# A graph layer's dense passes in plain fp32 instead of two 12-bit parts in float32r

## The chip, the cores and the metric

One core of one Trainium2 chip. The time is that of one launch in device microseconds; the kernel before was run three times.

## The reference

Two GraphSAGE layers, a linear layer, a residual and a layer norm, on 12500 nodes with 256 features and 200000 edges sorted by destination. The destinations are drawn as 12500 u^2, so the first nodes receive most edges.

```python
def _sage_conv(x, src, dst, W_l, b_l, W_r):
    msgs = x[src]
    agg = jax.ops.segment_sum(msgs, dst, num_segments=N_NODES)
    deg = jax.ops.segment_sum(jnp.ones((src.shape[0],), x.dtype), dst, num_segments=N_NODES)
    mean = agg / jnp.maximum(deg, 1.0)[:, None]
    return mean @ W_l + b_l + x @ W_r
...
h = jax.nn.relu(_sage_conv(x, src, dst, W1_l, b1, W1_r))
h = jax.nn.relu(_sage_conv(h, src, dst, W2_l, b2, W2_r))
out = _layernorm(x + (h @ W3 + b3))
```

## The kernel before

The sum over edges is made in two ways.

- **Hot nodes** (the first 1792 in layer one, 2304 in layer two) have so many edges that a dense product pays. For a range of destination nodes the kernel keeps a matrix of counts (how often node s sends to node d), in uint8, by source block: 98 blocks of 128 source nodes. `count` (line 881) builds it: DVE makes 0/1 matrices ("pick", line 908), TensorE multiplies them (lines 930 and 934), ACT or DVE copies the sums to the uint8 counts (lines 944 and 948). `products` (line 841) then runs a **pass**: for every source block, rows (features) as the stationary operand times the counts of 512 destination nodes, widened to 32 bits by ACT (`widened`, line 833), added up in two PSUM banks, `dense_ps` for the first 128 features and `beside_ps` for the others. A pass over 256 nodes (a half pass) uses one bank. Layer one has three full passes and a half one, layer two four and a half one.
- **The other nodes** are gathered: a **round** is four indirect DMAs on POOL's queue (line 286) of 128 rows each, and matmuls by 0/1 matrices that add the rows of a node (lines 298 and 314), added to a ring of sums by DVE (line 328). There are 474 rounds.

A **block** of 128 destination nodes whose sums are ready goes through the layer's own matmuls, which are plain fp32 with 256 columns (`sage`, lines 1123 and 1125; in layer two also line 1207 and the layer norm).

Precision of the passes: the rows are used as two float32r parts, the upper 12 bits of the mantissa (a bitwise and) and the rest. Layer one gets the parts from a stage of its own, `splitting` (line 784): x is loaded to the place of the counts not yet made, DVE splits two blocks at a time (lines 812 and 813), and the parts are stored to the DRAM tensor `x2_d`. Layer two gets them where a block of h is made: `exact` (lines 760 and 761) and a second store, to `h2_d`. `loaded` (line 775) brings one block's two parts, 256 KB, into one of five tiles. A block in a full pass is four matmuls: two parts, two halves of the features.

The order of the work is written out by a planner at build time. `layer` (line 645) goes through the rounds and gives each a room in us (5.05 in layer one, 5.0 in layer two); it fills a round with pieces of blocks and with dense work taken from a generator, each priced on PE, DVE and ACT, until the costliest engine has used up the room. Prices are written in the code, among them

```python
def product_cost(width):
    on_pe, on_act = (1.0, 0.62) if width == DN else (0.6, 0.33)
...
COST_DEGREES, COST_REST, COST_SPLIT = (0.5, 0.25, 0.0), (0.0, 0.0, 0.3), (0.0, 1.25, 0.0)
...
yield 1.75, 1.65, 1.1     # a block of the first layer: its own matmuls, DVE with the splitting, ACT
```

Each engine then runs its instructions in that order. `stages_1` and `stages_2` (lines 1055 and 1067) say which counting runs beside which pass; layer one ends with a pass alone, and layer two begins with one.

Of the kernel before, what the change touches and what calls it, by code (L numbers as in the profile page):

```python
# [8 lines left out]
F32 = mybir.dt.float32  # L9
F32R = mybir.dt.float32r  # L10
F16 = mybir.dt.float16
BF16 = mybir.dt.bfloat16
I32 = mybir.dt.int32
U16 = mybir.dt.uint16
U8 = mybir.dt.uint8
# [12 lines left out]
P = 128  # L28
# [23 lines left out]
def by_runs(  # L52
# [89 lines left out]
    h_d = dram.tile([NB * P, D], F32, name="h_d")  # L142
    x2_d = dram.tile([P, NB, 2, D], F32, name="x2_d")
    h2_d = dram.tile([P, NB, 2, D], F32, name="h2_d")
    CW = DN + WIDEST
# [471 lines left out]

    split = keep.tile([P, 2, 2, D], F32, name="split")
    assert NB * CW % 4 == 0
    counts_flat = [keep.tile([P, NB * CW], U8, name=f"counts{i}") for i in range(2)]  # L620
    counts = [t.rearrange("p (b d) -> p b d", b=NB) for t in counts_flat]

# [134 lines left out]

    def exact(t, s):

        nc.vector.tensor_scalar(s[:, 0].bitcast(I32), t.bitcast(I32), -4096, None, op0=OP.bitwise_and)  # L760
        nc.vector.tensor_tensor(s[:, 1], t, s[:, 0], op=OP.subtract)

    STREAMS = 4
# [8 lines left out]

    N2, WIDE = 5, 4

    def loaded(b, back, table):

        rows = rows_pool.tile([P, 2, D], F32, name="rows", bufs=N2)
        load = nc.sync.dma_start(rows, table[:, b])
        freed(load, back)
        if table is h2_d:  # L780
            tc.add_manual_dep(load.ins, rows_after, LANDED, reason="the first layer's last gathers")
        return rows

    def splitting():

        size = 2 * 2 * D
        bufs = NB * CW // 4 // size
        flat = counts_flat[1].bitcast(F32)
        raw = {}

        def fetched(u):
            t = flat[:, u // 2 % bufs * size:(u // 2 % bufs + 1) * size].rearrange("p (b k d) -> p b k d", b=2, k=2)
            whole = min(2, (N - u * P) // P)
            loads = []
            if whole < 2:
                left = N - (u + whole) * P
                nc.vector.memset(t[:, whole, 1], 0.0)
                loads.append(nc.sync.dma_start(t[:left, whole, 1], x[(u + whole) * P:N]))
            if whole:
                loads.append(nc.sync.dma_start(t[:, :whole, 1], x[u * P:(u + whole) * P].rearrange(  # L800
                    "(b p) d -> p b d", p=P)))
            if u < 2 * bufs:
                for load in loads:
                    tc.add_manual_dep(load.ins, strips[-1], LANDED, reason="the gathers' tables first")
            return t

        for b in range(0, NB, 2):
            for u in range(b, min(b + 2 * (bufs - 3), NB), 2):
                if u not in raw:
                    raw[u] = fetched(u)  # L810
            s = raw.pop(b)
            nc.vector.tensor_scalar(s[:, :, 0].bitcast(I32), s[:, :, 1].bitcast(I32), -4096, None, op0=OP.bitwise_and)
            nc.vector.tensor_tensor(s[:, :, 1], s[:, :, 1], s[:, :, 0], op=OP.subtract)
            nc.sync.dma_start(x2_d[:, b:b + 2], s)
            yield COST_SPLIT

# [16 lines left out]
    def widened(counted):  # L833
        wide = rows_pool.tile([P, DN], F32, name="wide", bufs=WIDE)
        if len(counted.shape) > 2:
            nc.scalar.copy(wide.rearrange("p (b d) -> p b d", b=2).bitcast(F32R), counted)
        else:
            nc.scalar.copy(wide.bitcast(F32R), counted)  # L838
        return wide

    def products(n0, width, counts_of, table, into):


        half = width < DN
        ps = [pool.tile([P, DN], F32, name=name)
              for pool, name in ((dense_pool, "dense_ps"), (beside_pool, "beside_ps"))[:width // 256]]
        if half:
            nc.tensor.matmul(ps[0], lhsT=zeros_b, rhs=steps[:, :DN], start=True, stop=False)
        rows, counted, wide = {}, {}, {}
        for b in range(0, NB, 2):  # L850
            for u in range(b, min(b + N2, NB)):
                if u not in rows:
                    rows[u] = loaded(u, b - (u - N2), table)
                    counted[u] = counts_of(u) if not half or u % 2 == 0 else None
            for u in range(b, min(b + 4, NB)):
                if u not in wide:
                    wide[u] = wide[u - 1] if half and u % 2 else widened(counted[u])
            for u in (b, b + 1):
                for k in range(2):
                    for c in range(NC):  # L860
                        own = rows[u][:, k, c * P:(c + 1) * P].bitcast(F32R)
                        if half:
                            a = u % 2 * width
                            nc.tensor.matmul(ps[0][:, c * width:(c + 1) * width], lhsT=own,  # L864
                                             rhs=wide[u][:, a:a + width].bitcast(F32R), start=False,
                                             stop=u == NB - 1 and k == 1 and c == NC - 1)
                        else:
                            nc.tensor.matmul(ps[c], lhsT=own, rhs=wide[u].bitcast(F32R),  # L868
                                             start=u + k == 0, stop=u == NB - 1 and k == 1)
# [127 lines left out]
    COST_DEGREES, COST_REST, COST_SPLIT = (0.5, 0.25, 0.0), (0.0, 0.0, 0.3), (0.0, 1.25, 0.0)  # L997

# [56 lines left out]
    def stages_1(waiting):  # L1055

        into = [rows_pool.tile([P, NC, 256], F32, name=f"sums_{i}", bufs=1) for i in range(2)]
        nc.vector.memset(counts[0][:, :, DN:], 0.0)
        yield [counting(3), (degrees(HOT1 // P), 12.0), (splitting(), NB // 2 * max(COST_SPLIT))]
        nc.vector.memset(counts[1][:, :, DN:], 0.0)  # L1060
        yield [passed(waiting, 1536, 256, held(0, 256), x2_d, into), counting(2),
               moving(count_d[1], counts[0][:, :, :256])]
        yield [passed(waiting, 1024, 512, held(1), x2_d, into), counting(1), moving(count_d[0], counts[1])]
        yield [passed(waiting, 512, 512, held(0), x2_d, into), counting(0)]
        yield [passed(waiting, 0, 512, held(1), x2_d, into)]

    def stages_2(waiting):

        into = sums_a, sums_b
        yield [passed(waiting, 512, 512, held(0), h2_d, into)]  # L1070
        yield [passed(waiting, 0, 512, held(1), h2_d, into), moving(counts[0][:, :, :256], count_d[1]), counting(4)]
        yield [passed(waiting, 1024, 512, streamed(count_d[0]), h2_d, into), counting(5)]
        yield [passed(waiting, 1536, 512, held(0), h2_d, into)]
        yield [passed(waiting, 2048, 256, held(1, 256), h2_d, into)]

# [73 lines left out]
    def first_block(b, agg=None):  # L1149
# [85 lines left out]
    nc.sync.dma_start(biases[:, 0], b2[None, :].to_broadcast([P, D]))  # L1235
    sums_a, sums_b = tables[:, :NC * 256].rearrange("p (c d) -> p c d", c=NC), split[:, 0]
    w3_sb = split[:, 1]
    nc.sync.dma_start(w3_sb, w3.rearrange("(c p) f -> p c f", p=P))
# [7 lines left out]

    layer(Gathers(h_d, True), last_block, 5, staged(stages_2), 5.0, 14)

# [368 lines left out]
```

## Time and profile before

| what | us |
|---|---|
| median of three runs | 3097.36 |
| lowest, highest | 3088.63, 3106.94 |
| the profiled execution | 3104.8 |
| its span in the trace | 3103.0 |

The mean granted clock of TensorE was 0.897. A row of a group gives the line, the engine, the operation, the tiles it writes and reads, their shapes and the count, then busy us and the mean ns of one, then the idle time of the engine just before them and what ended most of it. A matmul's record lasts from its start to its modelled end, so neighbours overlap. A row of waits gives who waited for whom: total us, times, longest.

### The profile page before, as it was taken

Reading aid. Unit: us, or ns where it says so; the run is one execution under the profiler, and the core shown is the slowest. Engines: PE = TensorE matmul, PEld = TensorE weight load, DVE = VectorE, ACT = ScalarE, POOL = GpSimd, SP = SyncE. Lnnn points to the kernel's source line nnn. Section 1 sums busy time; section 2 is a strip of 40 time slices with the busy share of each in tenths; the row PEclk is TensorE's granted clock in tenths of the full one; section 3 lists DMA queues with packets and bytes.
Section 4 is the critical chain, followed back from the end, with each engine's and each line's share of the span. In section 5 each row is a group of like instructions: output and inputs, shape, how many; then the busy total and the mean of one; then the engine's idle time right before and its main releaser. Section 6 shows DMA issues by size and latency. Waiting matters only on the chain.

```text
span 3103.0 us, 45692 instructions
## 1 busy us (share of the span) xinstructions
PE 2412.6 (78%) x13753; PEld 1604.2 (52%) x13753; DVE 1525.2 (49%) x4554; ACT 1384.4 (45%) x2794; POOL 1851.4 (60%) x1906
## 2 busy tenths in 40 slices
PE   3356888888878788888876888887888888887776
PEld 1123555555544555556554555554555566566644
DVE  6764766656666666643232124444444343344344
ACT  0236666666622666644332443554444423333321
POOL 6546666556655666656654665665666556666653
PEclk7567999999999999989988998998998899989988
DMA  4893877756655555567756875766677657677843
GB/s 116 301 348 109 260 228 232 252 183 200 188 183 164 174 165 177 170 187 245 241 178 198 258 229 177 219 215 184 209 226 230 192 173 219 212 222 236 263 130 90
DMA packets 366615, 634.88 MB, mean 205 GB/s; under 512 B 85371, under 2 KB 173081, under 8 KB 366361
## 3 DMA queue, kind: packets, MB, share of 16 engines
q1 hardware_dynamic: 271011, 382.42, 38.3%
q0 software_dynamic: 91008, 248.63, 26.7%
q8 instruction: 115, 1.88, 0.2%
q10 hardware_dynamic: 4342, 0.80, 0.2%
q14 instruction: 139, 1.14, 0.1%
HBM read 544.85 MB, written 86.78 MB: 204 GB/s over the span
## 4 chain that ended last, share of the span: by engine, by line
PE 63%; issue 9%; DVE 8%; another core or an unknown queue 7%; DMA 6%; ACT 5%; DVEq 1%; POOL 0%; ACTq 0%; SPq 0%; POOLq 0%
PE dense_ps L868 10%; PE beside_ps L868 10%; PE count_ps L930 9%; PE part_ps L298 8%; PE block_ps L1123 5%; PE block_ps L1125 5%; PE sum_ps L314 5%; PE block_ps L1207 3%; PE block_ps L1094 3%; ACT counts L944 3%; PE dense_ps L864 3%; PE count_ps L934 2%; DMA rows<-h_d 2%; DMA x_d<-counts 1%
## 5 line engine op out<-in xcount | busy, mean ns | idle before, releaser
L286 POOL DMA_INDIRECT got<-in_x_dram,src_t x988 | 983.6, 996 | 646.1 <-issue 241.3
L286 POOL DMA_INDIRECT got<-h_d,src_t x908 | 865.6, 953 | 573.9 <-issue 226.4
L930 PE MATMUL count_ps<-pick,low 128*128 128x490 bf16 x1360 | 453.8, 376 | 333.8 <-ACT counts L944 139.1
L944 ACT CAST counts<-count_ps 128x490 f32 (+2 forms) x852 | 581.2, 682 | 232.3 <-PE count_ps L934 52.4
L868 PE MATMUL dense_ps<-wide,rows 128*128 128x512 f32 x1372 | 637.7, 465 | 46.5 <-ACT wide L838 16.3
L868 PE MATMUL beside_ps<-wide,rows 128*128 128x512 f32 x1372 | 565.7, 412 | 0.0
L838 ACT CAST wide<-counts 128x512 fp32r<-128x512 uint8 x588 | 359.6, 621 | 455.8 <-PE beside_ps L868 188.9
L868 PEld LDWEIGHTS dense_ps<-wide,rows 128*128 128x128 f32 x1372 | 276.6, 202 | 187.3 <-issue 99.5
L908 DVE TENSOR_SCALAR pick<-steps,tables 128x686 bf16<-128x686 f16 (+3 forms) x792 | 319.0, 416 | 105.2 <-PE count_ps L930 38.6
L298 PE MATMUL part_ps<-got,one 128*32 128x257 f32 (+1 forms) x3792 | 331.7, 424 | 22.8 <-DMA got<-h_d,src_t 12.4
L930 PEld LDWEIGHTS <-low 128*128 128x128 bf16 x1360 | 152.0, 117 | 318.2 <-issue 161.6
L948 DVE CAST counts<-count_ps 128x196 f32 (+2 forms) x316 | 208.5, 660 | 179.8 <-PE count_ps L930 46.9
L868 PEld LDWEIGHTS beside_ps<-wide,rows 128*128 128x128 f32 x1372 | 275.8, 201 | 40.1 <-ACT split L876 0.3
L308 ACT COPY some<-part_ps 128x257 f32<-128x257 f32 (+1 forms) x340 | 127.0, 374 | 351.1 <-PE part_ps L298 102.9
L314 PEld LDWEIGHTS sum_ps<-two,some 128*128 128x128 f32 x1360 | 223.7, 215 | 89.4 <-issue 39.4
L242 DVE TENSOR_TENSOR one<-lo_t,lane_b 128x128 f32<-128x128 bf16 x474 | 134.8, 286 | 267.1 <-PE part_ps L298 81.6
L314 PE MATMUL sum_ps<-two,some 128*128 128x128 f32 x1360 | 238.7, 303 | 32.2 <-ACT some L308 12.8
L328 DVE TENSOR_TENSOR sums<-sums,sum_ps 128x256 f32 x340 | 139.7, 411 | 250.0 <-PE beside_ps L868 88.7
L1133 DVE TENSOR_TENSOR own<-block_ps,biases 128x256 f32<-128x256 f32 x196 | 82.9, 423 | 312.3 <-remote 101.8
L298 PEld LDWEIGHTS part_ps<-got,one 128*32 128x32 f32 x3792 | 78.5, 112 | 191.1 <-issue 167.9
L934 PE MATMUL count_ps<-aft,low 128*128 128x98 bf16 x659 | 169.0, 256 | 0.0
L1130 ACT COPY sums<-zero 128x256 f32<-128x256 f32 x164 | 66.4, 405 | 224.6 <-PE block_ps L1125 74.3
(199 smaller groups left out, 2904.8 us busy)
## 6 DMA issues: line engine op xcount, KB each, us to landing
rows<-h_d SPq DMA_DIRECT2D x490, 256.0 KB
rows<-x_d SPq DMA_DIRECT2D x392, 256.0 KB
x_d<-counts SPq DMA_DIRECT2D x49, 512.0 KB
h_d<-split SPq DMA_DIRECT2D x98, 256.0 KB
got<-in_x_dram,src_t POOLq DMA_INDIRECT x988
got<-h_d,src_t POOLq DMA_INDIRECT x908
h_d<-own SPq DMA_DIRECT2D x98, 128.0 KB
h_sb<-h_d SPq DMA_DIRECT2D x98, 128.0 KB
```

The lines of the kernel that those rows point to most:

```text
L286: rows = nc.gpsimd.indirect_dma_start(out=g[:, j, :D], out_offset=None, in_=self.table, in_offset=bass.IndirectOffsetOnAxis(ap=src_t[:, e: ...
L298: strip = nc.tensor.matmul(part_ps[j * W:(j + 1) * W, :width], lhsT=one[:, j], rhs=g[:, j, :width], start=r == 0, stop=r == n - 1)
L314: nc.tensor.matmul(sum_ps[:, c], lhsT=some[:, c * P:(c + 1) * P], rhs=two, start=True, stop=True)
L838: nc.scalar.copy(wide.bitcast(F32R), counted)
L868: nc.tensor.matmul(ps[c], lhsT=own, rhs=wide[u].bitcast(F32R), start=u + k == 0, stop=u == NB - 1 and k == 1)
L908: nc.vector.tensor_scalar(r[:, :w * NB], steps[:, :w * NB], key_t[g][:, t - lo_g:t - lo_g + 1], None, op0=OP.is_equal)
L930: nc.tensor.matmul(ps[:, :(b - a) * NB], lhsT=s, rhs=r[:, a * NB:b * NB], start=j == 0, stop=j == n_in - 1 and alone)
L934: nc.tensor.matmul(ps[:, :NB], lhsT=before[0], rhs=before[1], start=False, stop=True)
L944: copies.append(nc.scalar.copy(to[:, :, a:][:, :, bass.ds(off_act.at(t), b - a)], of).ins)
L948: beside.append(nc.vector.tensor_copy(to[:, :, a:][:, :, bass.ds(off_dve.at(t), b - a)], of).ins)
L1123: nc.tensor.matmul(ps[:, 1], lhsT=own_t[:, c], rhs=wr[:, c], start=c == 0, stop=c == NC - 1)
L1125: product = nc.tensor.matmul(ps[:, 0], lhsT=agg[:, c], rhs=wl[:, c], start=c == 0, stop=c == NC - 1)
```

## The change

All passes use x and h themselves, in fp32, against the counts widened to plain fp32. The stage `splitting`, `exact`, the tensors `x2_d` and `h2_d` and their stores go. `loaded` brings two blocks of 128 KB each at once, again into five tiles, from x or from `h_d`. A block in a full pass is two matmuls. The planner's prices and rooms are new. In layer two, sums and the last weights get tiles of their own in place of `split`.

```diff
-    def exact(t, s):
-        nc.vector.tensor_scalar(s[:, 0].bitcast(I32), t.bitcast(I32), -4096, None, op0=OP.bitwise_and)
-        nc.vector.tensor_tensor(s[:, 1], t, s[:, 0], op=OP.subtract)
...
-    N2, WIDE = 5, 4
-    def loaded(b, back, table):
-        rows = rows_pool.tile([P, 2, D], F32, name="rows", bufs=N2)
-        load = nc.sync.dma_start(rows, table[:, b])
-        freed(load, back)
...
+    PAIRS_IN, WIDE = 5, 4
+    def loaded(u, since, table):
+        rows = rows_pool.tile([P, 2, D], F32, name="rows", bufs=PAIRS_IN)
+        first = table is x
+        n_rows = N if first else NB * P
+        whole = min(2, (n_rows - u * P) // P)
...
+            loads.append(nc.sync.dma_start(rows[:, :whole], table[u * P:(u + whole) * P].rearrange(
+                "(b p) d -> p b d", p=P)))
+        for load in loads:
+            freed(load, since - (u - 2 * PAIRS_IN + 1))
...
-    def splitting():
...
-            nc.scalar.copy(wide.bitcast(F32R), counted)
+            nc.scalar.copy(wide, counted)
...
-            for u in range(b, min(b + N2, NB)):
+            for u in range(b, min(b + 2 * PAIRS_IN, NB), 2):
                 if u not in rows:
-                    rows[u] = loaded(u, b - (u - N2), table)
+                    rows[u] = loaded(u, b, table)
...
             for u in (b, b + 1):
-                for k in range(2):
-                    for c in range(NC):
-                        own = rows[u][:, k, c * P:(c + 1) * P].bitcast(F32R)
...
-                            nc.tensor.matmul(ps[c], lhsT=own, rhs=wide[u].bitcast(F32R),
-                                             start=u + k == 0, stop=u == NB - 1 and k == 1)
+                for c in range(NC):
+                    own = rows[b][:, u - b, c * P:(c + 1) * P]
...
+                        nc.tensor.matmul(ps[c], lhsT=own, rhs=wide[u], start=u == 0, stop=u == NB - 1)
...
-        on_pe, on_act = (1.0, 0.62) if width == DN else (0.6, 0.33)
+        on_pe, on_act = (0.87, 0.62) if width == DN else (0.45, 0.33)
...
-        nc.sync.dma_start(h_d[b * P:(b + 1) * P, :], h)
-        s = split[:, b % 2]
-        exact(h, s)
-        nc.sync.dma_start(h2_d[:, b], s)
-        yield 1.75, 1.65, 1.1
+        nc.sync.dma_start(h_d[b * P:(b + 1) * P, :], h)
+        yield 1.75, 0.9, 1.1
...
-        layer(gathers_1, first_block, 3, staged(stages_1), 5.05, 8)
+        layer(gathers_1, first_block, 3, staged(stages_1), 4.65, 8)
...
-    layer(Gathers(h_d, True), last_block, 5, staged(stages_2), 5.0, 14)
+    layer(Gathers(h_d, True), last_block, 5, staged(stages_2), 4.62, 14)
```

More of the change, by code (lines that the diff above doesn't have):

```diff
@@ L9 @@
 F32 = mybir.dt.float32
-F32R = mybir.dt.float32r
 F16 = mybir.dt.float16
@@ L616, in by_runs @@
     keep = ctx.enter_context(tc.tile_pool(name="keep", bufs=1))
[L618 to L621, printed above, removed]
+    sums_b = keep.tile([P, NC, 256], F32, name="sums_b")
+    w3_sb = keep.tile([P, NC, D], F32, name="w3_sb")
+    counts = [keep.tile([P, NB, CW], U8, name=f"counts{i}") for i in range(2)]
     HELD = [counts[1], counts[0], counts[1], counts[0], counts[0][:, :, 256:], counts[1]]
@@ L771, in freed @@
             tc.add_manual_dep(load.ins, strips[used[-n]], LANDED, reason="products done")
-    N2, WIDE = 5, 4
-    def loaded(b, back, table):
-        rows = rows_pool.tile([P, 2, D], F32, name="rows", bufs=N2)
-        load = nc.sync.dma_start(rows, table[:, b])
-        freed(load, back)
-        if table is h2_d:
-            tc.add_manual_dep(load.ins, rows_after, LANDED, reason="the first layer's last gathers")
-        return rows
-    def splitting():
[L786 to L815, printed above, removed]
@@ new lines, in by_runs @@
+    PAIRS_IN, WIDE = 5, 4
[4 more added lines that the diff above has]
+        whole = min(2, (n_rows - u * P) // P)
+        loads = []
+        if whole < 2:
+            left = n_rows - (u + whole) * P
+            nc.vector.memset(rows[:, whole], 0.0)
+            loads.append(nc.sync.dma_start(rows[:left, whole], table[(u + whole) * P:n_rows]))
+        if whole:
+            loads.append(nc.sync.dma_start(rows[:, :whole], table[u * P:(u + whole) * P].rearrange(
+                "(b p) d -> p b d", p=P)))
+        for load in loads:
+            freed(load, since - (u - 2 * PAIRS_IN + 1))
+            if not first:
+                tc.add_manual_dep(load.ins, rows_after, LANDED, reason="the first layer's last gathers")
+        return rows
@@ L835, in widened @@
         if len(counted.shape) > 2:
[L836 removed]
+            nc.scalar.copy(wide.rearrange("p (b d) -> p b d", b=2), counted)
         else:
[L838 removed]
+            nc.scalar.copy(wide, counted)
         return wide
@@ L850, in products @@
         for b in range(0, NB, 2):
-            for u in range(b, min(b + N2, NB)):
+            for u in range(b, min(b + 2 * PAIRS_IN, NB), 2):
                 if u not in rows:
-                    rows[u] = loaded(u, b - (u - N2), table)
+                    rows[u] = loaded(u, b, table)
+            for u in range(b, min(b + 6, NB)):
+                if u not in counted:
                     counted[u] = counts_of(u) if not half or u % 2 == 0 else None
@@ L858, in products @@
             for u in (b, b + 1):
-                for k in range(2):
-                    for c in range(NC):
-                        own = rows[u][:, k, c * P:(c + 1) * P].bitcast(F32R)
[L862 to L868, printed above, removed]
-                                             start=u + k == 0, stop=u == NB - 1 and k == 1)
+                for c in range(NC):
+                    own = rows[b][:, u - b, c * P:(c + 1) * P]
+                    if half:
+                        a = u % 2 * width
+                        nc.tensor.matmul(ps[0][:, c * width:(c + 1) * width], lhsT=own,
+                                         rhs=wide[u][:, a:a + width], start=False,
+                                         stop=u == NB - 1 and c == NC - 1)
+                    else:
+                        nc.tensor.matmul(ps[c], lhsT=own, rhs=wide[u], start=u == 0, stop=u == NB - 1)
                 used.append(len(strips))
@@ L1057, in stages_1 @@
         into = [rows_pool.tile([P, NC, 256], F32, name=f"sums_{i}", bufs=1) for i in range(2)]
[L1058 to L1061, printed above, removed]
+        for t in counts:
+            nc.vector.memset(t[:, :, DN:], 0.0)
+        yield [counting(3), (degrees(HOT1 // P), 12.0)]
+        yield [passed(waiting, 1536, 256, held(0, 256), x, into), counting(2),
                moving(count_d[1], counts[0][:, :, :256])]
-        yield [passed(waiting, 1024, 512, held(1), x2_d, into), counting(1), moving(count_d[0], counts[1])]
-        yield [passed(waiting, 512, 512, held(0), x2_d, into), counting(0)]
-        yield [passed(waiting, 0, 512, held(1), x2_d, into)]
+        yield [passed(waiting, 1024, 512, held(1), x, into), counting(1), moving(count_d[0], counts[1])]
+        yield [passed(waiting, 512, 512, held(0), x, into), counting(0)]
+        yield [passed(waiting, 0, 512, held(1), x, into)]
     def stages_2(waiting):
         into = sums_a, sums_b
[L1070 to L1074, printed above, removed]
+        yield [passed(waiting, 512, 512, held(0), h_d, into)]
+        yield [passed(waiting, 0, 512, held(1), h_d, into), moving(counts[0][:, :, :256], count_d[1]), counting(4)]
+        yield [passed(waiting, 1024, 512, streamed(count_d[0]), h_d, into), counting(5)]
+        yield [passed(waiting, 1536, 512, held(0), h_d, into)]
+        yield [passed(waiting, 2048, 256, held(1, 256), h_d, into)]
     def staged(stages):
```

7 lines of the change are left out of this document (2 added, 5 removed).

## The prediction

> **What bounds the kernel now.** I read the page first: busy shares, the slices, the chain, the groups.
>
> ```profile
> span 3103.0 us, 45692 instructions
> PE 2412.6 (78%) x13753; PEld 1604.2 (52%) x13753; DVE 1525.2 (49%) x4554; ACT 1384.4 (45%) x2794; POOL 1851.4 (60%) x1906
> PE   3356888888878788888876888887888888887776
> PEclk7567999999999999989988998998998899989988
> PE 63%; issue 9%; DVE 8%; another core or an unknown queue 7%; DMA 6%; ACT 5%; DVEq 1%; POOL 0%; ACTq 0%; SPq 0%; POOLq 0%
> ```
>
> PE is the busiest engine and carries 63% of the chain that ended last. From the fifth slice on it is level at seven to eight tenths: the planner spreads the dense work evenly over the gather rounds. Its idle time is 3103.0 - 2412.6 = 690 us. POOL, which paces the gathers, is itself waiting for PE; the list of waits says so, and says what PE waits for:
>
> ```profile
> POOL got L286 <- PE part_ps L298: 329.0, 126, 11.2
> PE count_ps L930 <- ACT counts L944: 139.1, 115, 8.1
> PE count_ps L930 <- issue: 89.8, 111, 7.2
> PE block_ps L1094 <- DVE own L1134: 41.9, 18, 4.9
> PE block_ps L1207 <- DVE own L1134: 34.7, 14, 5.6
> PE dense_ps L864 <- DMA rows<-h_d: 10.2, 8, 2.3
> PE dense_ps L868 <- DMA rows<-x_d: 7.1, 5, 2.6
> PE dense_ps L868 <- DMA rows<-h_d: 6.9, 9, 1.1
> ```
>
> (Total us, times, longest.) So a gather round takes as long as PE's work in it plus PE's handovers to ACT and DVE. Time added to PE counts, except where it fills a wait that it has anyway. The windows by stage (busy PE, PEld, DVE, ACT, POOL, granted clock, DMA share, GB/s) say where the waits lie:
>
> ```profile
> 0.00:200.00 200.00, 75.04 (x466) 37.34 (x467) 140.15 (x401) 39.07 (x65) 112.65 (x106) 0.65 0.74 252
> 588.00:844.00 256.00, 215.59 (x1264) 135.65 (x1257) 155.78 (x469) 175.35 (x320) 154.03 (x159) 0.96 0.63 192
> 1356.00:1481.00 125.00, 106.54 (x579) 74.31 (x570) 41.76 (x147) 48.80 (x113) 77.94 (x83) 0.95 0.76 239
> 2007.00:2263.00 256.00, 207.04 (x1118) 138.37 (x1111) 115.02 (x312) 118.31 (x235) 154.78 (x161) 0.91 0.66 202
> 3012.00:3103.00 91.00, 60.79 (x325) 39.92 (x323) 38.96 (x120) 19.17 (x55) 37.98 (x40) 0.84 0.33 97
> ```
>
> Of the 690 us idle, 125 lie in the first 200 us (setup, DVE the busy engine) and 30 in the last 91 (gathers alone): products cannot fill these. 535 us lie in between.
>
> **The change part by part: the products.** What a matmul holds PE for is read from starts, since a record's duration contains the drain behind it. The timeline (start, length, group) has both kinds:
>
> ```profile
> 1999.81 1.02 PE L1123 MATMUL block_ps<-w2r_sb,own_t 128*128 128x256 f32 x4
> 2000.67 1.03 PE L1125 MATMUL block_ps<-w2l_sb,sums 128*128 128x256 f32 x4
> ...
> 2008.78 0.40 PE L868 MATMUL dense_ps<-wide,rows 128*128 128x512 f32 x1
> ...
> 2009.93 0.40 PE L868 MATMUL beside_ps<-wide,rows 128*128 128x512 f32 x1
> ...
> 2790.04 0.72 PE L864 MATMUL dense_ps<-wide,rows 128*128 128x256 f32 x4
> ```
>
> and the groups, kept apart by shape, have the counts:
>
> ```profile
> L868 PE MATMUL dense_ps<-wide,rows 128*128 128x512 f32 x1372 | 637.7, 465 | 46.5 <-ACT wide L838 16.3 <-issue 12.1 <-DMA rows<-x_d 7.1
> L864 PE MATMUL dense_ps<-wide,rows 128*128 128x256 f32 x784 | 146.9, 314 | 14.2 <-DMA rows<-h_d 10.2 <-ACT wide L836 2.0 <-issue 1.9
> L1123 PE MATMUL block_ps<-w2r_sb,own_t 128*128 128x256 f32 x392 | 115.8, 422 | 33.7 <-DVE z L1209 18.3 <-issue 11.4 <-DVE one L242 2.3
> ```
>
> Lines 1123 and 1125 are plain fp32 matmuls already. The code issues 98 x 2 = 196 at line 1123 in the second layer and the trace has 392 records: two records for each plain fp32 matmul. Four records of 256 columns run from 1999.81 to 2000.67, 0.215 us each, so one plain fp32 matmul of 256 columns holds PE for 0.43 us. The 12-bit parts go as float32r, one record each (1372 = 7 passes x 98 blocks x 2 parts at the first half of the features): from 2008.78 to 2009.93 are five steps, 0.23 us for 512 columns. In the half passes four records take 0.72 us with the last 0.31 long, so (0.72 - 0.31)/3 = 0.14 us.
>
> A full block now costs 4 x 0.23 = 0.92 us. After, it is 2 matmuls x 2 records of 512 columns. No row shows plain fp32 at 512 columns. From below it could be 0.215 a record, were the step of line 1123 set by loading the weights rather than by the columns; from above it is twice 0.215, were it set by columns. I take 0.43, as 128-column plain fp32 steps are shorter:
>
> ```profile
> 1418.86 0.61 PE L314 MATMUL sum_ps<-two,some 128*128 128x128 f32 x4
> L314 PE MATMUL sum_ps<-two,some 128*128 128x128 f32 x1360 | 238.7, 303 | 32.2 <-ACT some L308 12.8
> ```
>
> Four records with weights of the same size are over in 0.61 us, the last 0.30 long, so a step is (0.61 - 0.30)/3, about 0.1: the columns set it, and it doubles with them. A block then costs 2 x 2 x 0.43 = 1.72 us, +0.80; x 7 passes x 98 = 686 blocks: +549 us. A half block costs 4 x 0.215 = 0.86 against 0.56, +0.30 x 196 = +59. Together +608 us at full clock; at the 0.93 between the windows' 0.96 and 0.91, **+654**. The planner does not see it: its price for a block falls from 1.0 to 0.87, so it still deals out products as if they were cheaper. In the built program's tensor queue the rounds where products stand alone (the end of layer one, the start of layer two) hold 4.8 to 5.5 wide matmuls, against 8 to 10.6 before: 4.1 to 4.7 us of PE instead of 1.8 to 2.4.
>
> **What of it fills waits.** PE's idle time before the counting matmuls is one row of the page:
>
> ```profile
> L930 PE MATMUL count_ps<-pick,low 128*128 128x490 bf16 x1360 | 453.8, 376 | 333.8 <-ACT counts L944 139.1
> PE count_ps L930 <- DVE pick L908: 48.0, 10, 22.8
> PE count_ps L930 <- ACT counts L944: 11.0, 7, 7.0
> PE count_ps L930 <- issue: 8.0, 4, 4.3
> PE count_ps L930 <- DVE counts L813: 4.1, 1, 4.1
> ```
>
> The rows below the first are of the first 200 us alone: 71 us of the 334. That leaves 263 in the middle: PE there waits for copies of the counts on ACT and DVE, which are 61 to 68% busy (588 to 844 us) and go on while PE multiplies. I take 85% of it as filled, 223. The other 535 - 263 = 272 us are mostly chains that begin at PE's own result (block sum, DVE's two operations, transpose): filled only as far as other products stand between. I take a third, 91. Bounds: nothing and all 535. Value: **-314**.
>
> **The clock.** The slices show the granted clock at 0.5 to 0.7 where PE is half idle, 0.8 to 0.9 later. With less idle time I take 0.95 for 0.925 in the middle: 2412.6 - 75.0 - 60.8 = 2277 us busy x (1 - 0.925/0.95) = **-60**. The bounds are no gain and a clock of 1.0: 2277 x (1 - 0.925) = 171, with the added work at 608 instead of 654, which makes the sum 157 us lower. I stay near the small end, because waits of 5 to 8 us are the longest of their rows and most of their kinds stay.
>
> The Trainium skill (TensorE: Matmul & The Clock Gate, Part 1) says that an idle window of about 3.4 us sends the clock to half, and that a busy one brings it back. The trace agrees where PE is idle longest, 0.65 in the first 200 us. By that rule the sum would move by the 157 us only if no wait of that length were left.
>
> **The rest.** The splitting stage goes:
>
> ```profile
> L812 DVE TENSOR_SCALAR counts<-counts x49: 401/427/679, 101.9 to 202.6; 128x512 int32<-128x512 int32 x49
> L813 DVE TENSOR_TENSOR counts<-counts x49: 670/684/753, 102.6 to 204.0; 128x512 f32<-128x512 f32 x49
> L761 DVE TENSOR_TENSOR split<-own,split x98: 402/416/485, 169.6 to 1654.8; 128x256 f32<-128x256 f32 x98
> ```
>
> 49 x (0.43 + 0.68) = 54 us of DVE from 102 to 205 us, where PE waits 48 us for DVE's picks. Bounds 0 and 54; I take **-20**, since setup remains on DVE. Splitting h (line 761 and the operation before it) lies on a DVE that is two fifths busy or less: nothing, at most 98 x 0.42 = 41. Loads:
>
> ```profile
> rows<-h_d SPq DMA_DIRECT2D x490, 256.0 KB
> rows<-x_d SPq DMA_DIRECT2D x392, 256.0 KB
> ```
>
> 882 loads of 256 KB become 441 of the same size, and five tiles hold ten blocks instead of five; SP also loses the stores of x2 and h2. PE's waits for rows, 10.2 + 7.1 + 6.9, go: **-24**. New is that a pair must land whole before its first block: at each of nine passes at worst the longest such wait, 2.6 us, 0 to 23, and I take 0, as a pass's first rows are asked for ahead. ACT's widening stays one cast a block; a copy to float32 instead of float32r has no row, and I take no difference.
>
> Sum: 3104.8 (the profiled execution, 1.8 beyond its span) + 654 - 314 - 60 - 20 - 24 = 3341. The profiled run lies 7 us above the median, so 3335.
>
> **The rivals.** (1) *The waits stay*: the handovers are serial, and filling them only moves them. Then 3104.8 + 654 - 44 = 3715. For it: all engines together often stand until one PE result arrives. Against: after setup ACT and DVE are under 70% busy in every stage shown. (2) *The added work disappears in the idle time*, and PE, now dense, keeps its clock: 3104.8 + 608 - 535 - 171 - 44 = 2963, faster. It needs the fill and the clock together to exceed 608 - 44 = 564 of the 706 there is. For it: PE's idle time is spread over all slices. Against: PE's waits for its own blocks' DVE results stay. (3) *Plain fp32 at 512 columns costs half of what I take*, the 0.215 a record that the planner's 0.87 implies: 0.86 a block for 0.92, -0.06 x 686 = -41; half passes at 0.45 for 0.56, -22; with -44, 2998. Against: the same planner prices a block's four 256-column fp32 matmuls at 1.75, which is the trace's 8 x 0.215. (4) *Nothing measurable*, the fill at its upper end and the clock halfway.
>
> **How the numbers follow.** The forecast with fills of 150 to 450 us (3190 to 3500) 0.58; rival 1 or near it (3500 to 3715) 0.17; a fill that leaves 3113 to 3190, 0.08; rival 2, 0.08; rival 3, 0.05; rival 4, 0.04. Slower by over 0.5% (about what a measurement of this kernel can tell from no change) 0.83, faster 0.13, within 0.04. The range leaves out rivals 2 and 3 and the upper end of rival 1: 3100 to 3570.
>
> **What would show it.** Right: lines of the products with 2744 records of 512 columns and 784 of 256 as before, starts 0.43 and 0.215 apart, PE's busy share above 85%, its idle time before the counting matmuls well below 334 us, no wait for rows, granted clock 0.92 or more, the product-only rounds the ones that lengthen most. Wrong: steps of 0.215 at 512 columns (rival 3); idle time still near 690 us (rival 1); under 250 us at a clock near 1.0 (rival 2).

## The result, and the profile after

The changed kernel takes 3193.8 us (four runs, 3191.0 to 3199.6) against 3102.2 us before on the same chip (four runs), a ratio of 1.030 [1.026, 1.035]. The sign was forecast; the size was 236 us over the profiled execution and came out at 95 (span 3197.7 after 3103.0). The time lies inside the range of 3100 to 3570, at its lower end.

The page after, span, busy time by engine, granted clock by slice and the chain by engine:

```profile
span 3197.7 us, 44181 instructions
PE 2869.2 (90%) x13753; PEld 1587.9 (50%) x13753; DVE 1464.3 (46%) x4308; ACT 1393.4 (44%) x2749; POOL 1849.1 (58%) x1906
PEclk7569999999999999999998999999999999999998
PE 82%; DVE 4%; issue 4%; ACT 3%; another core or an unknown queue 2%; DMA 1%; DVEq 0%; ACTq 0%; POOL 0%; POOLq 0%
```

PE's busy time rose by 457 us, its idle time fell from 690 to 3197.7 - 2869.2 = 328 us, and 457 - 362 = 95 is the whole difference. The chain went from 63% to 82% PE. The timeline (start, length, group) of a product-only stretch and two groups, apart by shape:

```profile
1500.03 1.02 PE L838 MATMUL dense_ps<-wide,rows 128*128 128x512 f32 x2
1500.89 1.02 PE L838 MATMUL beside_ps<-wide,rows 128*128 128x512 f32 x2
1501.75 1.02 PE L838 MATMUL dense_ps<-wide,rows 128*128 128x512 f32 x2
1502.61 1.02 PE L838 MATMUL beside_ps<-wide,rows 128*128 128x512 f32 x2
...
L838 PE MATMUL dense_ps<-wide,rows 128*128 128x512 f32 x1372 | 731.6, 615 | 7.8 <-ACT wide L807 7.8
L834 PE MATMUL dense_ps<-wide,rows 128*128 128x256 f32 x784 | 204.5, 391 | 1.3 <-issue 1.3
```

A pair of records starts every 0.86 us: 0.43 for a record of 512 columns, as taken. Waits for rows are gone from both groups. The page has PE's idle time before the counting matmuls, 154.0 us where it was 333.8:

```profile
L899 PE MATMUL count_ps<-pick,low 128*128 128x490 bf16 x1360 | 429.9, 367 | 154.0 <-ACT counts L913 49.1
```

Some of the waits that PE has left (total us, times, longest), and two windows of the middle (busy PE, PEld, DVE, ACT, POOL, granted clock, DMA share, GB/s):

```profile
PE count_ps L899 <- ACT counts L913: 49.1, 74, 3.3
PE count_ps L899 <- issue: 35.2, 53, 3.2
PE block_ps L1173 <- DVE own L1103: 22.9, 9, 4.5
PE block_ps L1063 <- DVE own L1103: 11.3, 8, 3.6
...
500.00:1000.00 500.00, 455.23 (x2163) 233.36 (x2162) 277.52 (x813) 246.52 (x450) 285.39 (x294) 0.98 0.43 125
2000.00:2500.00 500.00, 487.98 (x2154) 252.37 (x2153) 219.65 (x586) 231.79 (x442) 303.94 (x315) 0.99 0.55 162
```

The same two windows before:

```profile
500.00:1000.00 500.00, 413.40 (x2363) 259.77 (x2362) 313.18 (x941) 268.33 (x506) 298.78 (x308) 0.94 0.64 199
2000.00:2500.00 500.00, 409.84 (x2214) 277.81 (x2214) 218.25 (x593) 227.44 (x456) 304.22 (x317) 0.91 0.67 208
```

The longest waits in these rows fell from 5 to 8 us to 3 to 4.5. The granted clock (the number behind the last count) is 0.96 to 0.99 in the five windows of 500 us from 500 to 3000, where it was 0.89 to 0.95.

To compare kernels I split a span in three: PE's work at full clock (each record times the step measured for its kind), what stretches at half clock add to it, and the rest. The steps are read from the starts of neighbouring records, so the first two are estimates from the traces. Before: 1948, 238 and 917 us. After: 2573, 110 and 515. So 625 us of work were added, the clock gave back 128 and the idle rest 402.

### The profile page after: what moved, and what is told of

Its sections match the earlier page's. It is cut to its first block, busy times and chain, and to the rows that moved or that the text cites. A ratio compares the mean times of both kernels' runs of the same rounds, so it can differ in the third digit from the quotient of the medians.

```text
span 3197.7 us, 44181 instructions
## 1 busy us (share of the span) xinstructions
PE 2869.2 (90%) x13753; PEld 1587.9 (50%) x13753; DVE 1464.3 (46%) x4308; ACT 1393.4 (44%) x2749; POOL 1849.1 (58%) x1906
## 4 chain that ended last, share of the span: by engine, by line
PE 82%; DVE 4%; issue 4%; ACT 3%; another core or an unknown queue 2%; DMA 1%; DVEq 0%; ACTq 0%; POOL 0%; POOLq 0%
PE dense_ps L838 19%; PE beside_ps L838 18%; PE count_ps L899 8%; PE part_ps L295 8%; PE dense_ps L834 5%; PE block_ps L1092 5%; PE block_ps L1094 5%; PE sum_ps L311 5%; PE block_ps L1173 3%; PE block_ps L1063 3%; ACT counts L913 2%; PE count_ps L903 2%; PE sum_ps L317 1%; DVE counts L917 1%
## 5 line engine op out<-in xcount | busy, mean ns | idle before, releaser
L838 PE MATMUL dense_ps<-wide,rows 128*128 128x512 f32 x1372 | 731.6, 615 | 7.8 <-ACT wide L807 7.8
L838 PE MATMUL beside_ps<-wide,rows 128*128 128x512 f32 x1372 | 707.8, 598 | 0.0
L913 ACT CAST counts<-count_ps 128x490 f32 (+2 forms) x807 | 549.3, 681 | 220.9 <-PE count_ps L903 62.2
L807 ACT CAST wide<-counts 128x512 f32<-128x512 uint8 x588 | 361.6, 618 | 639.0 <-PE beside_ps L838 456.8
L899 PE MATMUL count_ps<-pick,low 128*128 128x490 bf16 x1360 | 429.9, 367 | 154.0 <-ACT counts L913 49.1
L295 PE MATMUL part_ps<-got,one 128*32 128x257 f32 (+1 forms) x3792 | 316.2, 406 | 25.5 <-DMA got<-h_d,src_t 12.2
L917 DVE CAST counts<-count_ps 128x196 f32 (+2 forms) x361 | 237.5, 658 | 214.6 <-PE count_ps L899 75.7
L838 PEld LDWEIGHTS dense_ps<-wide,rows 128*128 128x128 f32 x1372 | 229.9, 194 | 138.2 <-issue 115.1
L311 PE MATMUL sum_ps<-two,some 128*128 128x128 f32 x1360 | 220.3, 287 | 12.9 <-issue 7.0
L834 PE MATMUL dense_ps<-wide,rows 128*128 128x256 f32 x784 | 204.5, 391 | 1.3 <-issue 1.3
```

Of the source, the lines that this page charges most:

```text
L295: strip = nc.tensor.matmul(part_ps[j * W:(j + 1) * W, :width], lhsT=one[:, j], rhs=g[:, j, :width], start=r == 0, stop=r == n - 1)
L311: nc.tensor.matmul(sum_ps[:, c], lhsT=some[:, c * P:(c + 1) * P], rhs=two, start=True, stop=True)
L807: nc.scalar.copy(wide, counted)
L838: nc.tensor.matmul(ps[c], lhsT=own, rhs=wide[u], start=u == 0, stop=u == NB - 1)
L899: nc.tensor.matmul(ps[:, :(b - a) * NB], lhsT=s, rhs=r[:, a * NB:b * NB], start=j == 0, stop=j == n_in - 1 and alone)
L913: copies.append(nc.scalar.copy(to[:, :, a:][:, :, bass.ds(off_act.at(t), b - a)], of).ins)
```

## The experiments

The runs fall into four **comparisons**: e1 to e4, e5 to e8, e9 to e11, and f1 to f4. In each the kernels ran on one chip, with the kernel before beside them: 3096.5 us in the first and 3099.9 in the second, near enough to the 3102.2 beside the changed kernel to set their times side by side. My theory: the added PE work is what was forecast, but the idle time and the clock take in the first of it almost for nothing. The rivals: something else in the change paid (the halved row traffic, the missing splitting stage), or the order of the work.

**A ladder of PE work.** Matmuls by zeros into the same sums, and one rung below. First, two per block in the kernel before (e1):

```diff
                             nc.tensor.matmul(ps[c], lhsT=own, rhs=wide[u].bitcast(F32R), ...
+                            if k == 0 and not (u == NB - 1 and k == 1):
+                                nc.tensor.matmul(ps[c], lhsT=zeros_b, rhs=steps[:, :DN], start=False, stop=False)
```

> The kernel before, with a matmul by zeros of the same width added behind every matmul of the upper 12-bit part (two per block): 686 x 2 x 0.215 + 196 x 2 x 0.11 = 338 us more PE work, nothing else changed. Theory (idle time and clock take the first added work): idle shrinks and the clock rises together, so the first half costs little: 3100 to 3140. Rival (the prediction's fixed share, 0.46 us of time for each us of work): 3250 or more.

Then behind every product (the condition `k == 0` left out; e2):

> The kernel before, with a matmul by zeros behind every matmul of both parts: 677 us more PE work, about the changed kernel's 625, but rows are still loaded as two parts and the splitting stays. Theory (PE work, fill and clock alone explain the changed kernel): 3220 to 3290, granted clock 0.95 or more, idle near 330 to 380 us. Rival (the halved row traffic and the missing splitting paid for what the prediction missed, some 145 us): 3340 or more.

And without the products of the lower part (`for k in range(1)`; e3):

> The kernel before without the products of the lower 12-bit part (they are left out of the sums): 363 us less PE work, same loads. Theory: PE's idle time grows by nearly as much and the clock falls, so 3030 to 3100. Rival (a kernel bound by PE's work, us for us): 2800 or less.

Beside 3096.5 us before, they took 3154.0 (1.019 [1.014, 1.024]), 3353.2 (1.083 [1.077, 1.088]) and 3074.6 (0.992 [0.989, 0.995]). Busy time by engine in the pages of e3, e1 and e2, each under its span:

```profile
span 3084.2 us, 42150 instructions
PE 2203.9 (71%) x11989; PEld 1360.6 (44%) x11989; DVE 1518.5 (49%) x4554; ACT 1378.5 (45%) x2794; POOL 1856.6 (60%) x1906
...
span 3147.5 us, 49200 instructions
PE 2672.3 (85%) x15517; PEld 1643.6 (52%) x15517; DVE 1538.2 (49%) x4554; ACT 1404.9 (45%) x2794; POOL 1853.7 (59%) x1906
...
span 3349.7 us, 52693 instructions
PE 2983.4 (89%) x17263; PEld 1710.2 (51%) x17263; DVE 1545.7 (46%) x4554; ACT 1430.2 (43%) x2794; POOL 1845.8 (55%) x1906
```

PE's idle time is 880, 690 (before), 475 and 366 us; the mean granted clock 0.831, 0.897, 0.935 and 0.948. The first 363 us of work cost 22 us of time, the next 338 cost 57, the last 339 cost 199. So the price of PE work is no share here: it is nearly nothing while there are waits and a slow clock to use up, and grows to 0.6 us for each. The range expected for e1 was missed by 14 us at its upper end. e2's was missed by 63, and its 3353.2 us lie in the range of the rival (3340 or more), that something else in the change paid. It takes 159 us more than the changed kernel for 49 us more work by the same count. Part of that is the dummies themselves. The timeline of e2 (start, length, group) has a product followed by its dummy:

```profile
1501.17 0.58 PE L871 MATMUL beside_ps<-wide,rows 128*128 128x512 f32 x1
1501.60 0.39 PE L874 MATMUL beside_ps<-steps,zeros_b 128*128 128x512 f16 x1
1501.63 0.58 PE L871 MATMUL dense_ps<-wide,rows 128*128 128x512 f32 x1
1502.06 0.39 PE L874 MATMUL dense_ps<-steps,zeros_b 128*128 128x512 f16 x1
1502.09 0.58 PE L871 MATMUL beside_ps<-wide,rows 128*128 128x512 f32 x1
```

The pair holds PE for 0.46 us, a block of four pairs 1.84, against 1.72 in the changed kernel: over 686 blocks 82 us, not 49. Some 77 us remain for what else the change did; the runs on the row traffic and on the splitting stage, below, take these one at a time.

**One step further up**, the changed kernel with dummies behind its products (e7):

> The changed kernel with a matmul by zeros of the same width behind every product (686 x 2 x 0.215 + 196 x 2 x 0.11 = 338 us more PE work). Theory (the waits and the clock that could be had are used up): 270 to 330 us longer, 3465 to 3525, clock unchanged at 0.95. Rival (half of any added work still disappears): 3360 or less.

3441.4 us, 248 more for 338 us of work, 0.73 each, between the theory's 270 and the rival's 170. Idle fell by another 58 us, and the clock rose from 0.950 to 0.964 where it was expected unchanged. Even at 92% busy some of an addition was still taken in.

**The row traffic.** The changed kernel with its loads issued twice (e4):

```diff
+        again = rows_pool.tile([P, 2, D], F32, name="again", bufs=1)
...
+            loads.append(nc.sync.dma_start(again[:, :whole], table[u * P:(u + whole) * P].rearrange(
+                "(b p) d -> p b d", p=P)))
```

> The changed kernel, with every load of a pair of blocks issued a second time into a tile that nobody reads: the row traffic of the kernel before, PE's work unchanged. Theory: DMA is covered by now, so within 15 us of the changed kernel, 3190 to 3210. Rival (lighter DMA traffic shortened PE's handovers): 3240 or more, with PE idle back up by 50 us.

3202.1 us, 8 more than the changed kernel, its PE idle 340 us against 328. From 500 to 1000 us the DMA engines move 157 GB/s, against 125 in the changed kernel and 199 before, as the stores of the parts stay away. The lighter loads paid for next to nothing of the miss.

**The splitting stage**, put back into the changed kernel (its parts are stored and read by nobody; e5):

> The changed kernel with the splitting of x left in as a stage of the first 200 us (its parts are stored and read by nobody). Theory (the splitting stage, not the row traffic, is the part of the saving that the prediction put too low at 20 us): 3230 to 3260, with PE's busy time in the first 200 us back from 107 to about 76 us. Rival (setup is bound by other DVE work, and the stage is hidden): 3190 to 3215.

3278.4 us, 85 more and 18 above the expected range. But with a room of 4.65 the dense work of layer one no longer fitted into the rounds: some 57 of the planner's units were left for the last one. So again with a room of 4.79 (e10); that run belongs to the third comparison, below, where the kernel before takes 2610.5 us:

> The run with the splitting stage left in, with the room of layer one at 4.79 instead of 4.65, so that the planner's dense work ends inside the rounds (at 4.65 some 57 of its units were left over for the last one). Theory (the stage itself holds setup up, by DMA at a share of 1.04 in 100 to 200 us and by later counting): 3225 to 3255, so the stage costs the changed kernel 30 to 60 us and the rest of the 85 was overflow. Rival (all 85 were overflow): 3195 to 3210.

3072.7 us, against 3012.7 for the changed kernel in the fourth comparison (f2, below), where the kernel before takes 2610.3 us: the stage costs **60 us** there, not the 20 that I took. The expected times were for a kernel before at 3100 us and can't be held against this run; the expected cost, 30 to 60 us, holds. How much of e5's 85 us was overflow under its own conditions was not measured. The windows from 100 to 200 and 200 to 300 us (busy PE, PEld, DVE, ACT, POOL, clock, DMA share, GB/s), of e10 first and then of f2, show where PE falls behind:

```profile
100.00:200.00 100.00, 46.03 (x305) 22.76 (x304) 68.50 (x173) 34.81 (x59) 48.74 (x43) 0.59 1.03 389
200.00:300.00 100.00, 76.72 (x509) 42.66 (x509) 57.19 (x173) 69.90 (x125) 69.97 (x74) 0.82 0.57 176
...
100.00:200.00 100.00, 77.19 (x514) 35.98 (x513) 60.79 (x168) 59.23 (x98) 52.71 (x54) 0.66 0.26 75
200.00:300.00 100.00, 92.95 (x548) 62.00 (x549) 72.30 (x196) 68.20 (x121) 68.70 (x68) 0.95 0.65 179
```

With the stage PE has 47 us less done by 300 us, and in the second 100 us the DMA share is 1.03 at 389 GB/s, against 0.26 at 75. That DVE's work is the cost was my reason, and an experiment spoke against it: in the kernel before, ACT made the upper part (e8; the planner's price of the stage moves with it).

```diff
-            nc.vector.tensor_scalar(s[:, :, 0].bitcast(I32), s[:, :, 1].bitcast(I32), -4096, None, op0=OP.bitwise_and)
+            nc.scalar.copy(s[:, :, 0].bitcast(F32R), s[:, :, 1])
```

> The kernel before, with ACT instead of DVE making the upper part in the splitting stage (a copy that rounds to float32r), 49 x 0.43 = 21 us less DVE work in the first 200 us. Theory (DVE's work in the splitting stage lies on the path): 10 to 20 us shorter, 3080 to 3090. Rival (the stage is hidden or bound by its DMAs): 3093 to 3103.

3101.8 us beside 3099.9, a ratio of 1.001 [0.998, 1.003]: 21 us of DVE less, and nothing. Whether the stage's cost is its DMA, or that counting starts later behind it in the planner's order, was not told apart.

**The planner's prices.** The changed kernel with prices of 1.74 and 0.88 and rooms of 5.82 and 6.42 (e6):

> The changed kernel with the planner told what a block really holds PE for (1.74 and 0.88) and rooms of 5.82 and 6.42 so that the dense work still ends with the rounds; the same instructions in another order. Theory (PE's work is what the time follows, and evenly spread rounds fill more waits): 3130 to 3185, PE busy above 92%. Rival (the order is immaterial once PE is dense): 3185 to 3205.

3132.5 us: 61 us below the changed kernel, and still slower than before (1.010 [1.007, 1.014]). PE is busy for 91%, a little under the expected 92. The same PE work in another order was worth two thirds of what the change cost, so in this comparison part of the price of the change was the wrong price in its planner.

**A hybrid**, layer one plain and layer two in parts, in the third comparison (e9, and e11 with another room):

```diff
+        if plain:
+            return (1.74, 0.0, 0.62) if width == DN else (0.88, 0.0, 0.33)
...
+        plain = table is x
+        return (dense(waiting, (products_x if plain else products)(n0, width, counts_of, table, into)),
```

> Layer one of the changed kernel (x itself in plain fp32, no splitting stage, priced at 1.74 and 0.88, room 5.82), layer two of the kernel before (h as two float32r parts). PE work over the kernel before: 294 x 0.80 + 98 x 0.30 = 265 us. Theory (the first 300 us of added PE work cost about 50 us, and the missing stage gives 40 to 60 back): 3070 to 3110, about the kernel before. Rival (the fill differs by layer: layer one, with the counting beside the products, fills less): 3130 or more.

> The same with the room of layer two at 4.93 instead of 5.0, so that its products end with the rounds and not nine rounds earlier. Theory (rounds without products leave PE idle): 10 to 20 us below the hybrid. Rival (the gathers and blocks at the end fill those rounds anyway): within 5 us.

2791.8 and 2798.4 us, against **2610.5** for the kernel before in the same comparison: ratios of 1.070 [1.068, 1.072] and 1.072 [1.070, 1.074]. The hybrid's expectation failed: 181 us more for 265 us of work, where about nothing was expected. The room is worth nothing. The surprise was the kernel before itself, 16% faster than in the first two comparisons, with all its runs between 2609 and 2620 us. Its code and data were the same. The chip bore the same number, 7, as in the first comparison.

**What differed.** An engine tells the others that a result is ready by updating a semaphore for which they wait; this is called a release here. In the first trace of the kernel before, the timeline around one gather round has this:

```profile
1420.68 0.64 PE L298 MATMUL part_ps<-got,one 128*32 128x257 f32 x8
...
1423.45 0.37 ACT L308 COPY some<-part_ps 128x257 f32<-128x257 f32 x1 [1.99 <-PE beside_ps L868]
1423.45 0.29 DVE L242 TENSOR_TENSOR one<-lo_t,lane_b 128x128 f32<-128x128 bf16 x1 [1.63 <-PE beside_ps L868]
...
1423.69 0.94 POOL L286 DMA_INDIRECT got<-in_x_dram,src_t  x1 [1.38 <-PE beside_ps L868]
```

The matmuls at line 298 end at 1421.32. ACT's copy of their sums needs nothing else, and ACT is idle (the number in brackets); it starts at 1423.45, 2.1 us later, and DVE and POOL stand until about the same moment. The profile puts the wait down to a later matmul, since that was the last release that it saw. The trace's records of PE's semaphore show the release itself late: four matmuls that update it end from 1420.75 to 1422.77, no update is on record from 1420.0 on until 1423.43, and then three stand within 0.11 us. The latency from PE's end to the copy's start can be read for all copies at line 308 for which ACT was idle when PE ended. In the first trace, some 100 of them, it has a median of 0.12 us, an upper quartile of 1.17 and a 95th percentile of 2.2. Releases come late, in a quarter of the cases and by one or two us. To see whether that is what PE's idle time was made of, I ran the unchanged kernels again:

> The kernel before, unchanged, profiled again. Where the kernel before takes about 2610 us (as it did beside the hybrid), the theory (PE's idle time is mostly late releases: ACT starts its copy of a gather sum up to 2 us after PE is done) expects a latency of that copy of 0.12 us at the 95th percentile, PE idle about 400 us less than in the first profile, and a granted clock of 0.95 or more. Where it takes about 3100 us, both stay as in the first profile.

> The changed kernel, unchanged. Theory (the idle time that swallowed most of the added 625 us is late releases): with the kernel before at 2610 us there is little to fill, and the changed kernel takes 2950 to 3030, 13 to 16% more; at 3100 us it is 3% more, as before. Rival (the fill belongs to the kernel's order of work): 3% more in either case.

> The changed kernel with the planner's prices set right, again. Theory: 30 to 80 us below the changed kernel in either case, above the kernel before in either case.

> The kernel before with 677 us of matmuls by zeros, again. Theory: with the kernel before at 2610 us, 550 to 650 us more (nothing to fill, and the clock is high already); at 3100 us, 250 more as before.

Here too the kernel before took 2610.3 us. f1 took 2609.5; f2, the changed kernel, 3012.7, a ratio of **1.155** [1.153, 1.158]; f3 3016.0; f4 3215.6. The latency of the copy is 0.12 us at the 95th percentile in f1 and f2, and in all seven traces of the third and fourth comparisons; in the ten other traces it is 1.3 to 2.9. One copy, from f1's timeline, where the matmuls end at 1200.62, the update is on record at 1200.65 and the copy starts at 1200.73:

```profile
1199.97 0.65 PE L298 MATMUL part_ps<-got,one 128*32 128x257 f32 x8
...
1200.73 0.38 ACT L308 COPY some<-part_ps 128x257 f32<-128x257 f32 x1 [0.70 <-PE part_ps L298]
```

Span, busy time, clock and chain of the page of f1, then the first three of f2:

```profile
span 2609.6 us, 45692 instructions
PE 2248.2 (86%) x13753; PEld 1519.9 (58%) x13753; DVE 1527.1 (59%) x4554; ACT 1407.5 (54%) x2794; POOL 1866.1 (72%) x1906
PEclk8567899999999999999999899999999999999998
PE 57%; DMA 12%; DVE 7%; ACT 5%; issue 5%; POOL 3%; DVEq 1%; ACTq 0%; SPq 0%; POOLq 0%
...
span 3011.4 us, 44181 instructions
PE 2802.8 (93%) x13753; PEld 1560.5 (52%) x13753; DVE 1460.7 (49%) x4308; ACT 1399.3 (46%) x2749; POOL 1853.7 (62%) x1906
PEclk7579999999999999999999999999999999999999
```

The chain's 7% of "another core or an unknown queue" is gone, PE's idle time in the kernel before is 361 us instead of 690, and its clock 0.950 instead of 0.897. The clock and the latency came out as f1's theory has them. The idle time fell by 329 us, not by about 400, so that it was mostly late releases is not borne out: 361 us of it stay without them. The split into work, clock and rest:

| | work at full clock | half clock adds | rest | span |
|---|---|---|---|---|
| before, releases late | 1948 | 238 | 917 | 3103 |
| after, releases late | 2573 | 110 | 515 | 3198 |
| before, releases on time | 1948 | 76 | 586 | 2610 |
| after, releases on time | 2573 | 50 | 388 | 3011 |

With releases on time the same 625 us of work cost 402: there are 224 us of clock and waits to take in instead of 530. The rival (3% in either condition) fell. f3 missed: the priced order, worth 61 us where releases are late, is worth nothing (3 us more) where they are on time. That the order helps by putting work under the late releases fits this and is not shown otherwise. f4's 605 us were within what was expected. f2 was as its theory has it, and f4 with f2 repeats what e2 showed: 203 us more than the changed kernel for some 80 us more work.

Why releases come late in one comparison and not in another is open. The runs show it in whole comparisons, in all kernels of one alike, and twice the row traffic hardly added to it (upper quartile of the latency 1.03 us in e4, 0.90 in the changed kernel). The traces show one thing more. In the ten with late releases 24 to 31% of the updates of PE's semaphore have no record (2808 records for 3839 updating instructions in the first trace); in the seven others it is under 1% (3824 for 3839 in f1). The engine that the profile names as the end of a wait is inferred from these records, so in the traces with late releases these names are less sure than the idle times. Every time here is of an execution of which such records were taken, and whether taking them has a part in the lateness was not tried.

No kernel here beats the kernel before with the same arithmetic. Leaving out the lower part (e3) gains 0.8% and computes something else.

## Why the prediction was right in sign and wrong in size

- **The work added: right.** 0.43 and 0.215 us a record, 608 us taken, 625 by the later count; a record of the half passes before holds PE for 0.12 us rather than 0.14. Rival 3, half that, fell at the first timeline.
- **The clock: the step that failed.** The sum has -60 us for the clock (0.95 for 0.925 in the middle) and charges the added work at 0.93, 46 us more: together -14. By the split the clock gave back 238 - 110 = 128. From 500 to 3000 us the trace before has 391 us at half clock and the trace after 102, and the mean clock there is 0.96 to 0.99. Busy time rose by 457 us instead of the 654 - 60 = 594 of the sum. These 137 us are nearly the whole error of 141: 114 of them are the clock; some 40 are busy time beyond work and clock (227 us before, 186 after), the ends of records, more of which now overlap with the next one; the work, 625 instead of 608, took 17 back. The other end of my own bound, -171 and the work at 608, gives +437. I stayed at the small end because of the waits of 5 to 8 us and because "most of their kinds stay"; kinds stayed, but became shorter and fewer. The ladder shows clock and idle time moving together at each rung.
- **What the clock follows** can be read from the traces. It is granted in steps of 3.41 us, full or half. In the traces before and after, f1 and f2, full clock fell to half only after a step of which PE's records cover 0.66 or less (medians 0.30 to 0.41; not every step between 0.43 and 0.66 did it), and half went back to full after a step covered to 0.84 or more. The half-clock stretches fell from 98 (639 us) to 36 (320 us), and only 12 of the 98 and 1 of the 36 begin after a step without any PE work. The Trainium skill (TensorE: Matmul & The Clock Gate, Part 1), with its idle window of about 3.4 us, pointed to the better end of my bound. The trace agrees with the length of that window, 3.41 us, and not with its being idle: several short waits in one step bring half clock as well.
- **The fill: right in sum by luck, wrong in parts.** 314 + 20 + 24 = 358 us were to go from PE's idle time; 362 went. The waits before the counting matmuls fell from 334 to 154 us; 44 us of the 154 lie in the first 200 us, so in the middle these waits went from 263 to 110 us: 153, not 223. All waits of the first 200 us went from 125 to 92: 33, where I took 20. The others gave 176, not 91 + 24. Chains that begin at PE's own result were thought hardly fillable. That engines "often stand until one PE result arrives" I had before me and used as a point for rival 1; that such a wait can be a late release and not the chain's own work did not occur to me. How much of the 176 us that is was not measured.
- **The rest.** The splitting stage was worth 60 us, with releases on time, where I took 20, and not for the reason given (DVE). The row traffic was worth 8 in the one run that put it back. Splitting h was put at nothing because DVE was read as two fifths busy or less; 77 of its 98 operations lie between 200 and 1500 us, where DVE is busy for 54 to 63%. No run has it alone.
- **The planner's price** I named and did not charge: it was worth 61 us in the condition of the forecast.
- **The rivals.** Rival 1 (610 us more) is excluded in both conditions. Rival 2 (2963 us) was the better guide for the clock and failed on the 328 us of idle time that stayed. Rival 4, nothing measurable, fell by the ratio of 1.030 [1.026, 1.035].

The forecast's +236 lies between the +95 of one condition and the +402 of the other, by chance. Its mechanism, added work less what idle time and clock take in, describes both; how much there is to take in was not the kernel's own.

## What to carry to other kernels

Price an addition on the busiest engine in three parts (work at full clock, clock, idle time), and let the clock follow how densely PE works: in the traces before and after, half clock came only after a step of 3.41 us with PE at work for 0.65 of it or less, so short waits close together can cost it as one long wait does, and filling them gives it back. Before counting on idle time as a cushion, look whether an idle engine starts well after the work that it needs has ended; such idle time belongs to the conditions of the run, and a change that hides in it (3% here) can cost five times as much (15.5% here) where it is missing. A planner that deals out work by price has to be given the new price with the new work.

## What the runs showed of the hardware

- One kernel, one input: 3100 us beside the changed kernel and in two comparisons, 2610 in two others, each within 1%. Durations of single operations are the same (ACT's copy at line 308: 374 and 376 ns), the release between engines is not: 0.12 us at the 95th percentile, or 1.2 us and more in a quarter of the cases (first trace).
- A plain fp32 matmul appears as two records, which hold PE for 0.11 us each at 128 columns, 0.215 at 256 and 0.43 at 512. Float32r takes one record, of 0.23 us for 512.
- The granted clock was only ever full or half in the records, in steps of 3.41 us; its mean over a kernel went from 0.83 (e3) to 0.97 (f2) with the work that PE had to do. In the traces before and after, f1 and f2 it fell to half only after a step of which PE's records covered at most 0.66.
